# A four-layer graph network: 128-node spans at multiples of 64 for the segment sums, the tail's branch moved ahead of the last batch norm, and the routing check moved into layer 3

## The chip, the core and the metric

The kernel is one program on one core of a Trainium2 chip. Its time is the device time of one execution in microseconds (us). The core has five engines that run side by side, each on its own list of instructions in order: TensorE (PE, matmuls), VectorE (DVE), ScalarE (ACT), GpSimd (POOL), and SyncE (SP, which issues DMAs). Matmuls write PSUM, which has eight banks of 128 partitions x 512 float32 numbers; an engine must read a bank out before it is used again.

## The reference, cut to what matters

There are 3125 nodes with 256 features each and 50000 edges, sorted by destination. Four layers follow each other, and each has the same two lines:

```python
xn = layernorm(x)
x  = x + gnn(xn, edges) + mix(xn)      # a sum over the edges, and a dense mixer
x  = x + ffn(layernorm(x))             # a mixture of experts
```

- `gnn` of layer 0 sums `xn[src] @ rel_W[type]` over the edges into each destination and divides by the degree. Layer 1 is graph attention with 4 heads of 64 features: each edge's row `h[src]` is multiplied by a softmax weight before the sum. Layer 2 sums `value * h[col]`, then a batch norm over the nodes and a ReLU. Layer 3 sums `x[src]`, divides by the degree, adds a second product, makes each row's length 1, and again ends in a batch norm over the nodes and a ReLU.
- `ffn` of layer 3, called the tail here, has its own graph of 2048 nodes and 32768 edges (nodes of the first 16 tiles below). A small graph attention over it (4 heads of 4) gives scores, whose best two of four make the weights `g` of four experts: `out += g * (gelu(x @ W1[e] + b1[e]) @ W2[e] + b2[e])`, 256 to 512 to 256 features. Nodes outside of that graph get their scores without a sum.

All arithmetic is float32.

## The kernel before

**Tiles and chunks.** The nodes lie in 25 tiles of 128 (`T`; tile groups of four and a last of one, `GROUPS`). `self.x`, `self.xn` and `self.xnT` hold all nodes in SBUF. The edges lie in 391 chunks of 128 (`C1`), the tail's in 256 (`C2`). Since they are sorted by destination, the destinations of chunk c lie near node 8c.

**A segment sum.** `seg_near` (layers 0, 2 and 3) goes through the chunks. For each it issues on POOL one indirect DMA, which gathers 128 rows by their source index (L447), and for the chunk some places earlier it calls `to_tiles`. That makes on DVE a one-hot matrix E of edges by destinations (`one_hot`, L416, with the weight in it L418) and multiplies E with the gathered rows on PE (L430), adding up in a PSUM bank named `seg`, one for each node tile. `near(c)` gives the tiles in which a chunk's destinations can lie: one tile for ten chunks of each sixteen, two for the other six. With two tiles E is 128x256 and there are two matmuls. When a tile's last chunk is through, `close` reads the bank. So 391 chunks take 535 matmuls and the tail's 256 take 346. `gat_near` does the same for attention (layer 1 and the tail): its gather is L842, the softmax weights are made on DVE and ACT for sixteen chunks at a time (`att` L806, exp L834), and the gathered rows are multiplied by them in place (`ring`, L854) before the matmul. A float32 matmul has two records in the profile.

**Order.** POOL's list is in the order of the program (a manual schedule); the other engines' lists are made by a scheduler, which goes by estimated times and keeps to the dependences. `drive` interleaves generators, so many steps of each in turn: the segment sum of each layer is driven beside the layer's `mix`. `Banks` splits the eight PSUM banks among names; layer 0's and layer 1's sums have three `seg` banks, layers 2 and 3 and the tail have two.

**Batch norm.** `close` of layers 2 and 3 writes each tile's sum to DRAM (`c_h`) and adds up its statistics in `bn_tile` (L940 to L954). `bn_end` makes from them scale and shift. `bn_apply` then goes through the tile groups: it loads a group's sums into a buffer `bn_h` (L984, one buffer for each group), multiplies, adds, applies ReLU and adds to `x` on DVE (L986 to L989), and calls `norm_tiles`: statistics (L174), the reciprocal root on ACT (L139), `xn` on DVE (L178), transposes on PE and their evacuation into `xnT` (L165, L117, L119).

**Around the tail.** `route_check` tests on the device whether the tail's edges, which the kernel itself has sorted while layers 1 and 2 run, are spread evenly enough for `near`; it runs between layer 2 and layer 3. Its answer `ok` is read as a branch: `tail_regular` or `tail_general`. The branch stands after layer 3's `bn_apply`. `tail_regular` then:

- makes the experts' generator (`l3_near_ffn`, which loads the weights when it is first advanced),
- runs `breaks`, which loads each edge's neighbours in the sorted list (`dh`, sixteen small DMAs of SP, L753) and makes two masks from them (`pen`, `penc`, L755 to L761),
- runs `l3_near_setup`: the product with `W_gat` for all 25 tiles, the two attention scores of each node, a table of rows written to DRAM for the gathers (`l3rows`), and sixteen scatters on POOL that put each node's score where its first edge is (`l3seed`, L357),
- runs `spread`, which reads `l3seed` back (`sh`) and copies each score to all edges of its node (`se`, `pre`) in a scan,
- sets the weights of tile groups 16, 20 and 24, for which no sum is needed (`gate`), and takes 20 steps of the experts,
- drives the tail's `gat_near` and the experts side by side. An expert's first product (`hT`, with Gelu on ACT, L2192) needs only `xnT`; its second is added to `x` with the weight (L2200), so it waits for the group's gate. Bias rows come in after a group's four experts (L2206 to L2211). Group 12 to 15 comes last.

Two DMAs at the very end store `x` (L2625 to L2627).

**The prologue** makes all tiles' norms (`norm_x`), then the table `h_tab` group by group (`fill`), with the check of the edge list (`regular`) ahead of the fourth group's fill.

## Time and profile before

| what | value |
|---|---|
| median of 14 runs | 5123.6 us (5109.94 to 5148.38) |
| the profiled execution's own time | 5134.22 us |
| its span | 5132.4 us |
| mean granted TensorE clock | 0.812 of full speed |
| busy time, PE / DVE / ACT / POOL | 3752.1 / 2205.1 / 749.9 / 2579.8 us |
| first and last gather, layer 0 | 148.3 and 747.5 us |
| first and last gather, layer 1 | 1248.5 and 1849.9 us |
| first and last gather, layer 2 | 2399.5 and 2972.3 us |
| first and last gather, layer 3 | 3683.3 and 4332.9 us |
| first and last gather, tail | 4476.9 and 5016.6 us |

The profile is of one execution, which took 10.6 us more than the median. Its times count from the span's start. PE's busy time counts a matmul as busy at whatever clock it ran, so a stage in which the clock was low looks busier than the same work at full clock. An indirect DMA's row on POOL is the time in which POOL writes its descriptors, not the time until the data is there. "Remote" or "an unknown queue" as what ended a wait stands for a DMA's or another queue's event that the profile does not name.

### The profile page before, as it was taken

Reading aid. Unit: us, or ns where it says so; the run is one execution under the profiler, and the core shown is the slowest. Engines: PE = TensorE matmul, PEld = TensorE weight load, DVE = VectorE, ACT = ScalarE, POOL = GpSimd, SP = SyncE. Lnnn points to the kernel's source line nnn. Section 1 sums busy time; section 2 is a strip of 40 time slices with the busy share of each in tenths; the row PEclk is TensorE's granted clock in tenths of the full one; section 3 lists DMA queues with packets and bytes.
Section 4 is the critical chain, followed back from the end, with each engine's and each line's share of the span. In section 5 each row is a group of like instructions: output and inputs, shape, how many; then the busy total and the mean of one; then the engine's idle time right before and its main releaser. Section 6 shows DMA issues by size and latency. Waiting matters only on the chain.

```text
span 5132.4 us, 47098 instructions
## 1 busy us (share of the span) xinstructions
PE 3752.1 (73%) x13977; PEld 2534.5 (49%) x13977; DVE 2205.1 (43%) x7451; ACT 749.9 (15%) x1455; POOL 2579.8 (50%) x2605
## 2 busy tenths in 40 slices
PE   7778755863866766665866658998688995288888
PEld 3456543542444544343555434555465774256555
DVE  3465421125666784575434342112645222624333
ACT  2000001110100111112201011222121220012112
POOL 0475664664677635433666613662255555235440
PEclk9888876985877877877878767999798997588779
DMA  3432323213433320012333320000233233200000
GB/s 127 130 91 80 92 75 108 93 48 104 128 94 99 93 67 16 14 49 61 95 93 96 97 65 5 9 14 25 71 88 99 82 89 91 75 5 8 7 7 27
DMA packets 231200, 348.62 MB, mean 68 GB/s; under 512 B 74128, under 2 KB 168135, under 8 KB 230936
## 3 DMA queue, kind: packets, MB, share of 16 engines
q0 software_dynamic: 108384, 219.50, 15.7%
q1 hardware_dynamic: 118136, 121.97, 7.6%
q10 hardware_dynamic: 4416, 4.01, 0.2%
q8 instruction: 118, 1.93, 0.2%
q14 instruction: 146, 1.20, 0.1%
HBM read 294.62 MB, written 50.61 MB: 67 GB/s over the span
## 4 chain that ended last, share of the span: by engine, by line
PE 60%; DVE 16%; another core or an unknown queue 9%; issue 9%; DMA 3%; ACT 1%; POOL 1%; SPq 1%; DVEq 0%; POOLq 0%; ACTq 0%
PE mm L110 34%; PE seg L430 18%; DVE E L416 1%; PE mm L165 1%; DVE ring L854 1%; DVE ln_st L174 1%; PE mm L945 1%; DVE r_m L2041 1%; PE bn L954 1%; DVE xn L178 1%; PE mm L1362 1%; PE ga L812 0%; PE acc L1076 0%; DVE E L418 0%
## 5 line engine op out<-in xcount | busy, mean ns | idle before, releaser
L430 PE MATMUL seg<-G,E 128*128 128x256 f32 (+1 forms) x3210 | 886.4, 424 | 174.5 <-issue 67.2
L430 PEld LDWEIGHTS seg<-G,E 128*128 128x128 f32 x3210 | 664.1, 213 | 363.3 <-issue 151.5
L110 PE MATMUL mm<-xnT,w 128*128 128x512 f32 (+1 forms) x1232 | 554.4, 596 | 26.8 <-issue 19.7
L416 DVE TENSOR_SCALAR E<-iota_row,e1dl 128x128 f32<-128x128 f32 (+1 forms) x1173 | 363.4, 325 | 480.1 <-PE seg L430 256.1
L357 POOL DMA_INDIRECT by_src<-rec,place x391 | 395.0, 1010 | 337.0 <-PE mm L110 236.2
L447 POOL DMA_INDIRECT G<-h_tab,gi x391 | 383.4, 981 | 353.3 <-DMA selfw<-in_L_gnn_self_W 136.5
L430 PE MATMUL seg<-ring,E 128*128 128x264 f32 (+1 forms) x1762 | 450.4, 396 | 129.7 <-DVE E L416 55.3
L447 POOL DMA_INDIRECT G<-tab,e1src x391 | 379.8, 971 | 271.0 <-PE seg L430 155.7
L842 POOL DMA_INDIRECT ring<-l1rows,e1src x391 | 422.2, 1080 | 180.4 <-issue 68.3
L447 POOL DMA_INDIRECT G<-tab,e3src x391 | 387.9, 992 | 190.3 <-issue 74.5
L110 PE MATMUL mm<-w,hT 128*128 128x256 f32 (+1 forms) x1712 | 427.8, 403 | 19.2 <-ACT hT L1550 10.3
L430 PEld LDWEIGHTS seg<-ring,E 128*128 128x128 f32 x1762 | 325.3, 224 | 233.2 <-DVE E L416 82.6
L842 POOL DMA_INDIRECT ring<-l3rows,e2src x256 | 247.8, 968 | 293.0 <-PE seg L430 194.3
L357 POOL DMA_INDIRECT by_dst<-rec,place x256 | 251.6, 983 | 276.3 <-PE mm L110 213.4
L110 PEld LDWEIGHTS mm<-w,hT 128*128 128x128 f32 (+1 forms) x1712 | 328.1, 198 | 88.7 <-issue 18.9
L110 PEld LDWEIGHTS mm<-xnT,w 128*128 128x128 f32 x1232 | 241.4, 210 | 258.1 <-issue 241.2
L165 PE MATMUL mm<-ident,xn 128*128 128x128 f32 x400 | 97.1, 402 | 247.5 <-DVE xn L178 204.6
L418 DVE TENSOR_SCALAR E<-iota_row,e3dl,rec 128x128 f32<-128x128 f32 (+1 forms) x391 | 140.2, 385 | 271.1 <-PE seg L430 123.0
L1710 DVE SCALAR_TENSOR_TENSOR x<-mm,l2t_r,x 128x256 f32<-128x256 f32 x150 | 69.5, 481 | 330.3 <-PE mm L110 287.3
L165 PEld LDWEIGHTS mm<-ident,xn 128*128 128x128 f32 x400 | 68.1, 197 | 277.9 <-DVE xn L178 156.6
L854 DVE TENSOR_TENSOR ring<-ring,ex 128x260 f32<-128x260 f32 (+1 forms) x647 | 191.8, 319 | 3.5 <-ACT ex L834 2.7
L1703 ACT ACTIVATE h<-mm,b 128x512 f32<-128x512 f32 (+1 forms) x168 | 107.1, 641 | 393.6 <-PE mm L110 372.0
(710 smaller groups left out, 5096.1 us busy)
## 6 DMA issues: line engine op xcount, KB each, us to landing
w<-in_L_ffn_w SPq DMA_DIRECT2D x16, 1024.0 KB
h_tab<-htab_s SPq DMA_DIRECT2D x25, 512.0 KB
r_b<-rowa SPq DMA_DIRECT2D x64, 128.0 KB
bn_h<-c_h SPq DMA_DIRECT2D x50, 128.0 KB
G<-h_tab,gi POOLq DMA_INDIRECT x391
by_src<-rec,place POOLq DMA_INDIRECT x391
ring<-l1rows,e1src POOLq DMA_INDIRECT x391
G<-tab,e3src POOLq DMA_INDIRECT x391
```

What stands on the lines that cost most here:

```text
L110: m = self.nc.tensor.matmul(out, l, r, start=(i == 0), stop=(i == last))
L165: self.nc.tensor.transpose(p[:, i * P:(i + 1) * P], src(t0 + i)[:, k * P:(k + 1) * P], self.ident)
L174: nc.vector.bn_stats(st[:, t, :], self.x[:, t, :])
L357: return self.nc.gpsimd.indirect_dma_start(out=table, out_offset=bass.IndirectOffsetOnAxis(ap=idx, axis=0), in_=src, in_offset=None, bound ...
L416: self.nc.vector.tensor_scalar(e[:, :w], self.iota2[:, :w], g["dl"][:, c:c + 1], None, op0=OP.is_equal)
L418: self.nc.vector.tensor_scalar(e[:, :w], self.iota2[:, :w], g["dl"][:, c:c + 1], weight[:, c:c + 1], op0=OP.is_equal, op1=OP.mult)
L430: self.nc.tensor.matmul(A[t], e, rows_c, start=first, stop=last)
L447: nc.gpsimd.indirect_dma_start(out=ring[i % len(ring)][:, :D], out_offset=None, in_=table, in_offset=bass.IndirectOffsetOnAxis(ap=gidx[:, ...
L842: nc.gpsimd.indirect_dma_start(out=ring[:, i % RING].rearrange("p h f -> p (h f)"), out_offset=None, in_=table, in_offset=bass.IndirectOff ...
L854: nc.vector.tensor_mul(r[:, :, :d + 1], r[:, :, :d + 1], ex[:, c, :, None].to_broadcast([P, 4, d + 1]))
L1703: nc.scalar.activation(o[:, f, :n], p, AF.Relu, bias=b[:, 2 * e + f:2 * e + f + 1])
L1710: nc.vector.scalar_tensor_tensor(self.x[:, t, :], p, r[:, t, e:e + 1], self.x[:, t, :], op0=OP.mult, op1=OP.add)
```

## The change

1. **Spans.** `to_windows` takes the place of `to_tiles` for the sums without a weight (layers 0, 1, 3 and the tail; layer 2 stays as it is). A chunk is given one span of 128 nodes that starts at a multiple of 64 (`window`). E is always 128x128, and there is one matmul for each chunk: 391 or 256. Spans that start at a tile's first node are copied whole from PSUM to SBUF by ACT (`W_own`); those between are copied in two halves to the two tiles' `W_side`, and DVE adds own and side for every tile before `close`. A stage has 49 spans, the tail 31. The tests of the edge lists go by the same spans. Layer 0's sums have four `mm` and two `seg` banks, layer 1's two and two.
2. **Batch norm.** `bn_apply` loads into `xn` itself, and its `norm_tiles` normalises and evacuates on ACT. This holds for layers 2 and 3.
3. **The tail.** The branch now stands ahead of layer 3's `bn_end`; both arms do the batch norm themselves. In `tail_regular`, `bn_apply` takes the groups in the order 16, 20, 24, 0, 4, 8, 12, and after each group comes that group's part of the setup (`fill`: one product with a weight of 24 columns that gives the rows and both scores, ACT copies, the rows' DMA and the scatters) and, for the first three, its gate. Twelve expert steps come after the groups, forty more after `spread`. The last group's expert products do not wait for its gate: they go to `y` in `xn` with the bias, and four weighted additions for each tile follow the gate. Each group is stored when it is done.
4. **The check.** `route_check` is a third generator beside layer 3's sum and mix.
5. **The prologue** takes each group's norm just ahead of the previous group's `fill`; the check comes one group later.

The core of the diff:

```diff
+    def to_windows(self, pool, g, c, rows_c, A, w, close):
+        k = window(c, nt)
+        t = k // 2
+        nc.vector.tensor_scalar(e, self.iota_row, g["dl"][:, c:c + 1], None, op0=OP.is_equal)
...
+        nc.tensor.matmul(A["sum"], e, rows_c, start=(c == 0 or window(c - 1, nt) != k), stop=last)
...
+        if k % 2 == 0:
+            A["own"] = pool.tile([P, w], F32, name="W_own", bufs=2)
+            nc.scalar.copy(A["own"], acc)
+        else:
...
+            nc.scalar.copy(side[64:], acc[:64])
+            nc.scalar.copy(A["side"][:64], acc[64:])
+            own = A.pop("own")
+            nc.vector.tensor_add(own, own, side)
+            close(t, own)
-                self.to_tiles(pool, g, c, r.rearrange("p h f -> p (h f)"), A, 4 * f, close)
+                self.to_windows(pool, g, c, r.rearrange("p h f -> p (h f)"), A, 4 * f, close)
...
-            sums = dict(mm=3, acc=2, seg=3)
+            sums = dict(mm=4, acc=2, seg=2)
-                with Banks(self, mm=1, acc=2, ga=2, seg=3), tp("mix1") as mp:
+                with Banks(self, mm=2, acc=2, ga=2, seg=2), tp("mix1") as mp:
...
-        for t0, n in GROUPS:
-            h = pool.tile([P, n, D], F32, name=f"bn_h{t0}")
+        for t0, n in order:
+            h = self.xn[:, t0:t0 + n, :]
...
-            self.norm_tiles(t0, n)
+            self.norm_tiles(t0, n, True)
+            if then is not None:
+                then(t0, n)
...
     def tail_regular(self, sorted_r, bn, gb):
             experts = self.l3_near_ffn(fp, r, ready)
+            sc, sh = self.bn_end(bn, fp, *gb)
             pen, penc = self.breaks(gp, self.dlin2, C2)
...
+                def then(t0, n):
+                    fill(t0, n)
+                    if t0 >= T2:
+                        gate(t0, n)
+                self.bn_apply(bn, sc, sh, then, GROUPS[4:] + GROUPS[:4])
-                for _ in range(20):
+                for _ in range(12):
                     next(experts)
+            with tp("spread4") as p:
+                end(p, penc)
+            for _ in range(40):
+                next(experts)
...
-                while t0 not in ready:
+                while t0 not in ready and not last:
                     yield
...
+                    if last:
+                        nc.vector.tensor_add(y[:, e, i, :], p, b2r[:, e * D:(e + 1) * D])
...
-                with tp("chk4") as p:
-                    self.route_check(p, by_dst, ok4)
...
-                              (self.l3_mix(mp, self.xnT), 1))
+                              (self.l3_mix(mp, self.xnT), 1), (self.route_check(cp, by_dst, ok4), 1))
...
-                self.norm_x()
                 for i, (t0, n) in enumerate(GROUPS):
-                    if i == 3:
+                    self.norm_tiles(t0, n)
+                    if i:
+                        fill(*GROUPS[i - 1])
+                    if i == 4:
                         ok = self.regular(p, self.g)
-                    fill(t0, n)
+                fill(*GROUPS[-1])
```

## The prediction

> **What bounds it now.** I read the page first, then POOL's waits for each edge stage, then engine windows by stage, and for the tail the chain of waits.
>
> The page: span, the chain that ended last, and the two groups that the spans touch most (count | busy us, mean ns of one | idle before).
>
> ```profile
> span 5132.4 us, 47098 instructions
> PE 60%; DVE 16%; another core or an unknown queue 9%; issue 9%; DMA 3%; ACT 1%; POOL 1%; SPq 1%; DVEq 0%; POOLq 0%; ACTq 0%
> PE mm L110 34%; PE seg L430 18%; DVE E L416 1%; PE mm L165 1%; DVE ring L854 1%; DVE ln_st L174 1%; PE mm L945 1%; DVE r_m L2041 1%; PE bn L954 1%; DVE xn L178 1%; PE mm L1362 1%; PE ga L812 0%; PE acc L1076 0%; DVE E L418 0%
> L430 PE MATMUL seg<-G,E 128*128 128x256 f32 (+1 forms) x3210 | 886.4, 424 | 174.5 <-issue 67.2
> L447 POOL DMA_INDIRECT G<-h_tab,gi x391 | 383.4, 981 | 353.3 <-DMA selfw<-in_L_gnn_self_W 136.5
> ```
>
> PE carries 60% of the chain and segment sums 18% (0.18 x 5132 = 924 us). Two records make a matmul, so 3210 records are 3 stages x 535 matmuls, at 886.4/1605 = 0.55 us each. A gather holds POOL about 0.98 us, and 0.3 us lie before the next one (issue), so 391 cannot take less than about 391 x 1.25 = 489 us. Layer 0's gathers took 747.5 - 148.3 = 599 us, layer 1's 602, layer 3's 650: each stage is a mixture of a gather floor and of PE.
>
> POOL's waits (total us, times, longest): 148 to 760, 1248 to 1850, 3683 to 4345 and 4408 to 5060 us, in this order.
>
> ```profile
> POOL G L447 <- PE seg L430: 83.2, 88, 19.8
> ...
> POOL ring L842 <- PE seg L430: 45.4, 62, 9.0
> ...
> POOL G L447 <- PE seg L430: 155.7, 118, 8.2
> ...
> POOL ring L842 <- PE seg L430: 194.3, 36, 69.6
> ```
>
> Here gathers wait for PE to free ring buffers: layer 3 most, layer 1 little. These waits cap what fewer matmuls can give to a stage.
>
> Windows (window, length, busy us of PE, PEld, DVE, ACT, POOL, then granted clock).
>
> ```profile
> 600.00:780.00 180.00, 105.57 (x381) 81.17 (x380) 52.17 (x180) 2.93 (x12) 112.42 (x118) 0.73 0.27 76
> 3940.00:4200.00 260.00, 260.00 (x1016) 191.58 (x1015) 68.95 (x216) 69.60 (x111) 139.89 (x148) 1.00 0.29 84
> 4408.00:4526.00 118.00, 40.93 (x168) 33.98 (x168) 36.75 (x175) 7.61 (x15) 53.10 (x53) 0.57 0.25 60
> ```
>
> Layer 3's middle is PE alone (260 of 260 us at clock 1.00); layer 0's end is gathers (PE 105.6 of 180, clock 0.73); the tail's start is nobody (PE 40.9 of 118).
>
> The chain around the tail (start, us, what).
>
> ```profile
> 4339.84 4.10 PE seg L430 x19
> ...
> 4358.16 3.89 DMA bn_h<-bn_h
> ...
> 4372.50 1.28 DVE xn L178 x4
> ...
> 4421.26 6.43 DMA l3seed<-neg
> 4427.76 26.18 issue
> ...
> 4475.54 2.06 DMA l3seed<-sdst,sidx
> ...
> 4492.93 15.84 PE mm L110 x48
> 4508.77 17.26 issue
> 4526.02 13.98 PE mm L110 x37
> ```
>
> From 4349 to 4526 us the chain is latencies: batch norm, masks, a serial setup, sixteen scatters (4454 to 4475.5), the first expert, and a stop until DVE's `att` has its gathers. Then PE is busy 522 of 592 us. The profiled run is 5134.2 us (span plus 1.8), 10.6 above the median of 5123.6; I sum against 5134.2 and take 10.6 off at the end.
>
> **The change part by part.**
>
> *Spans, what they remove and add.* Each 391-chunk stage loses 144 matmuls, the tail 90. At full clock one costs 4.10/19 x 2 = 0.43 us. E shrinks, from 366 to 302 ns for those 144: DVE saves 9 us. Added per stage: 25 whole and 24 split copies on ACT, 73 in all, and 25 additions on DVE. Nearest rows: ACT 128x256 COPY from PSUM 372 ns, DVE `ring` product 319 ns; so ACT gets 27 us over 600 us, of which it used 24 of 632 in layer 0 and 59 of 602 in layer 1, and DVE 8. Both lie beside other work, unless a bank waits (rival below). Bounds of one handover: 0 to about 2 us.
>
> *Layer 0.* About 99 of the 144 matmuls fall in the first 270 chunks, where PE waits are; the rest lie in the gather-bound end. 99 x 0.48 (between 0.43 and 0.55) = 47, and I count 85%: -40. Ends: -20 (half hidden by gathers) and -60 (most of the 83.2).
>
> *Layer 1.* 391 gathers of 1.08 plus 0.3 us are 540 of 602 us. Waits for PE's sums are 45.4 and for E 10.9; I take half of the former: -22, ends -5 and -45.
>
> *Layer 3.* 107 of the 144 fall where PE is full: 107 x 0.44 = 47. The check ahead of the stage goes: POOL's first memset waited 16.5 us on `ok`. Its work now stands in the stage on DVE and PE, so I count 8 of it. Total -55, ends -30 and -75 (below half of the 155.7).
>
> *Batch norms.* A group of `bn_apply` took 7.04 us of DVE (4372.50 to 4379.14 and so on: three passes of about 1.12, four statistics, four `xn` at 0.32 spacing, `xnT` 0.69). With `xn` and `xnT` on ACT DVE keeps 5.05. Layer 2: 6.25 x 2 = 12.4 us, and a few more since loads need no closed pool: -15, ends -8 and -20. ACT takes 0.416 us for a 128x256 ACTIVATE where DVE takes 0.407: four are 1.7 and two evacuations of 0.586 1.2 us, under DVE's 5.05, which hides them. Without that cover ACT would bound the group at 2.9 us plus any table load (1.283 us in this trace), still less than 5.05.
> The Trainium skill, "ScalarE: Activation LUTs", section "Rules for kernel authors", says to use VectorE and not ScalarE for additions and products, up to three times as fast in bf16, which speaks against this step; by it the batch norm term would turn to a loss of several us. The float32 rows above (0.416 against 0.407) do not show it, so I go by the rows.
>
> *Prologue.* PE idled between the norms' transposes from 9 to 31 us, and fills now stand in there; the check (72.8 to 91 us) still follows. -5, ends 0 and -10.
>
> *Tail start.* Layer 3's end is 4349.4 us. After it SP's list has three row loads, sixteen `dh` loads (0.63 us of issue each, two buffers, so SP waits for DVE's masks, which stand behind `bn_end`) and only then the first `xn` load, behind which all groups wait. So I put DVE's first group 10 us later than now: 23 instead of 13 us after layer 3's end. Seven groups at 5.05 are 32 us, against 4407 now: about even. The gain comes behind that: masks, `W_gat`'s product (4424 to 4445), `neg` (6.4), `sidx` (4453.7) and most of the scatters now lie beside the groups. Twelve scatters can go under the groups, four follow (4 x 1.3), then the round trip of `l3seed` and `sh` (2 + 5.5) and the scans. First gather about 4442 instead of 4476.9: -35, ends 0 (SP's list holds everything) and -50. Behind the waiting `att` on DVE stand the experts' additions, as now; so PE stops again until gather 35 (46 us after the first), but two experts (15.8 + 13.8) are done by then, not one: -14.
>
> *Tail, rest.* 90 matmuls fewer: the small ones took 0.31 us (108.3 us for 346), at 0.27 for the part at full clock -24. Last group's bias steps (5113.1 to 5118.9) shrink to four short additions on DVE: -4. PE's idle 71 of 592 us, with the gate stall of 4 at 5065: -12, ends 0 and -25. Final store 5118.9 to 5132.4, 13.5 us for 3072 KB, becomes 128 KB: near the 3.9 us of the `bn_h` load, so -9. Tail: -35 - 14 - 24 - 4 - 12 - 9 = -98, ends -60 and -135.
>
> *Sum.* -5 - 40 - 22 - 15 - 55 - 98 = -235. 5134.2 - 235 = 4899; less 10.6, 4889 us by the median. Sum of the ends: -123 and -345, that is 5000 and 4779.
>
> A second rule speaks against the spans. The Trainium skill, "TensorE: Matmul & The Clock Gate", section "Part 1: The HAM clock gate", says the array runs at half clock after an idle window of some 3.4 us. The windows agree in kind (clock 1.00 at 3940 to 4200, 0.73 at 600 to 780). By the rule alone, PE with less to do in the gather-bound parts idles more and the saving there is eaten; the terms above already take little there.
>
> **Rivals.**
>
> *Gathers take over.* PE's waits shrink, but the queue's own time and the gathers' latency show up in their place: "an unknown queue" is 9% of the chain, and 47% of it in layer 0's last 180 us. Then layers 0, 1 and 3 give -20, -5 and -30, and the tail without an earlier start -60: with -20 in the prologue and layer 2 -135, 4989 us. Against it: the 155.7 and 83.2 us of waits on PE.
>
> *Slower: evacuation holds the banks.* Two `seg` banks, and ACT frees them in order behind Gelu (0.687 us), Exp batches with table loads (1.283 us) and statistics. If a span's bank is late, PE's whole list stands, experts and mixer with it. 3 x 49 + 31 = 178 spans. The saving of 235 is used up from 235/178 = 1.3 us a span, a queue of two Gelus or one load on ACT each time; at 2 us a span (356 us) the kernel is 121 slower, 5245 us. For it: ACT's list is shared with the mixers, 35.2 of 200 us busy at 3740 to 3940. Against it: ACT is 15% busy, and a span lasts eight chunks, some 10 us, while only one bank is being read.
>
> *The tail does not move.* The list on SP, and the experts behind all norms, make its start as late as now or 10 us later; then -98 becomes about -45, the total -182, 4942 us.
>
> *It does not do what it says.* A span test that fails sends the program to the general arms, far slower. With the reference's inputs the sorted destinations of each chunk of 128 lie 0 to 115 nodes behind their span's start (0 to 127 in the tail), so the tests should hold; 1 in 100.
>
> **Chances.** Forecast 0.62 (4830 to 4950), the tail alone not moving 0.12, gathers taking over 0.14, banks and other losses 0.11, general arm 0.01. A measurement of this kernel can tell about 0.2%, 10 us. Faster by more: 0.62 + 0.12 + 0.14 = 0.88; of the 0.12 left I give 0.01 to the same and 0.11 to slower. The range reaches from near the better ends (4800) to just past the gather rival (5005); outside are the two losing cases and a little at each end.
>
> **What would show it.** Right: 391 and 256 matmuls a stage in the sums' groups; POOL's waits on `seg` at a third of now in layer 3, with that stage 45 to 60 us shorter and layer 1's only some 20; first tail gather about 93 us after the last batch norm matmul of layer 3 (127 now); two experts done ahead of `att`; the last chain piece a small store. Wrong: PE's `seg` waiting for ACT copies by the span; layer 0 still near 599 us; the first `xn` load over 30 us after layer 3's end; or a layer 1 that lengthens because its additions on DVE delay the `ring` products.

## The result, and the profile after

The changed kernel takes 5160.9 us (median of 10 runs, 5150.92 to 5186.44); the kernel before, in the 47 runs that go with them, 5122.23 us. The ratio is 1.0085, interval 1.0065 to 1.0104: slower by 39 us, where 4889 us, a gain of 235, had been forecast. The profiled execution took 5171.95 us at a mean clock of 0.793.

The page of the changed kernel: the span, the chain by engine, and the two groups that answer to those shown of before.

```profile
span 5170.2 us, 45299 instructions
PE 55%; DVE 18%; another core or an unknown queue 11%; issue 10%; DMA 3%; ACT 2%; POOL 0%; SPq 0%; DVEq 0%; ACTq 0%; POOLq 0%
L459 PE MATMUL seg<-G,E 128*128 128x257 f32 (+1 forms) x1564 | 473.7, 443 | 202.0 <-DVE E L455 83.7
L494 POOL DMA_INDIRECT G<-tab,e1src x391 | 379.8, 971 | 507.7 <-PE seg L459 230.0
```

The matmuls are gone as announced: 1564 records are 782 matmuls for layers 0 and 3, 391 each, and the group costs 473.7 us. PE's share of the chain fell from 60% to 55%. The time went elsewhere: "an unknown queue" rose from 9% to 11%, DVE from 16% to 18%, and layer 3's gathers now wait on `seg` far longer than before. POOL's waits in the four edge stages show that (layer 0, layer 1, layer 3, tail; total us, times, longest):

```profile
POOL G L494 <- PE seg L459: 89.5, 80, 18.1
...
POOL ring L892 <- PE seg L459: 57.6, 73, 11.6
...
POOL G L494 <- PE seg L459: 230.0, 104, 21.6
...
POOL ring L892 <- PE seg L459: 144.4, 32, 26.8
```

Before, these were 83.2, 45.4, 155.7 and 194.3. Fewer matmuls did not shorten the first two. In layer 3 the wait grew by 74 us and its longest one from 8.2 to 21.6 us. Windows of the stretches that answer to those of before:

```profile
600.00:780.00 180.00, 101.33 (x290) 66.02 (x288) 50.39 (x184) 11.28 (x34) 108.48 (x115) 0.65 0.26 72
3940.00:4200.00 260.00, 212.62 (x720) 144.89 (x721) 51.14 (x175) 63.68 (x110) 106.89 (x113) 0.88 0.23 65
4384.00:4487.00 103.00, 54.23 (x196) 39.24 (x196) 62.89 (x262) 35.58 (x87) 22.73 (x25) 0.54 0.37 105
```

In layer 0's end PE did less and was granted less clock (0.65 against 0.73). In layer 3's middle, where PE had been busy 260 of 260 us, it is busy 212.6 of 260 at clock 0.88: PE now stands idle in a stretch where it had been busy throughout. The tail's start (layer 3's end to the first gather) is 103 us of mixed work instead of 118.

The stages, first to last gather and what lies between, in the two profiled executions:

| stretch | before, us | after, us | change | forecast |
|---|---|---|---|---|
| to the first gather | 148.3 | 136.0 | -12.3 | -5 |
| layer 0 gathers | 599.2 | 601.0 | +1.8 | -40 |
| up to layer 1 | 501.0 | 505.4 | +4.4 | 0 |
| layer 1 gathers | 601.3 | 607.0 | +5.7 | -22 |
| up to layer 2, layer 2 gathers | 1122.5 | 1122.1 | -0.4 | 0 |
| batch norm, experts, check, up to layer 3 | 710.9 | 666.2 | -44.7 | -15 - 8 |
| layer 3 gathers | 649.6 | 728.3 | +78.7 | -47 |
| up to the tail's first gather | 144.0 | 116.3 | -27.7 | -35 |
| tail gathers | 539.7 | 593.5 | +53.8 | -14 - 24 - 12 |
| last gather to the end | 115.8 | 94.5 | -21.3 | -4 - 9 |

Four stretches gain 106 us together, layer 3 and the tail's gathers lose 132, layers 0 and 1 give nothing.

The experiments came in five calls, each on one chip, and the chips are of two kinds. On that of the result and that of calls 2 and 3 (one chip; before: 5122, 5069 and 5073 us) PE's signals to the other engines often come late: of the signals that the trace records, 18% in after and 15% in before arrive over 1 us after the start of the last matmul record that sends one. On those of calls 1, 4 and 5 (three chips; before: 4596, 4597 and 4593 us) that share is 0.5 to 0.7%. They are called late and prompt chips below.

What the engines do takes the same time on both kinds: a gather 0.95 us and 0.30 us to the next, a run of twelve chunks on PE 5.34 us (shown below for after and h_after), a DMA packet during layer 3's gathers 0.118 us on average in after and 0.114 in h_after. What differs is when a waiting engine goes on. The mean granted clock differs too (before: 0.81 to 0.82 on late chips, 0.85 to 0.86 on prompt ones). The share of late signals is a rough measure: the traces of late chips record only 84 to 87% of PE's signals and 70 to 76% of DVE's and ACT's, those of prompt chips over 99%. So on a late chip "issue" or "remote" can also stand for a release that was not recorded.

### The profile page after: what moved, and what is told of

Read it like the earlier page. It is cut to its first block, busy times and chain, and to the rows that moved or that the text cites. A ratio compares the mean times of both kernels' runs of the same rounds, so it can differ in the third digit from the quotient of the medians.

```text
span 5170.2 us, 45299 instructions
## 1 busy us (share of the span) xinstructions
PE 3613.1 (70%) x12927; PEld 2352.3 (45%) x12927; DVE 2167.5 (42%) x7507; ACT 879.5 (17%) x1815; POOL 2586.3 (50%) x2609
## 4 chain that ended last, share of the span: by engine, by line
PE 55%; DVE 18%; another core or an unknown queue 11%; issue 10%; DMA 3%; ACT 2%; POOL 0%; SPq 0%; DVEq 0%; ACTq 0%; POOLq 0%
PE mm L116 33%; PE seg L459 10%; PE seg L443 4%; DVE E L455 2%; DVE ring L904 1%; PE mm L171 1%; DVE ln_st L180 1%; PE mm L995 1%; DVE r_m L2093 1%; PE bn L1004 1%; PE ga L862 1%; PE mm L1414 1%; DVE r_oha L2052 0%; DMA G<-h_tab,gi 0%
## 5 line engine op out<-in xcount | busy, mean ns | idle before, releaser
L459 PE MATMUL seg<-G,E 128*128 128x257 f32 (+1 forms) x1564 | 473.7, 443 | 202.0 <-DVE E L455 83.7
L116 PE MATMUL mm<-xnT,w 128*128 128x512 f32 (+1 forms) x1232 | 567.6, 610 | 23.0 <-issue 14.2
L455 DVE TENSOR_SCALAR E<-iota_row,e1dl 128x128 f32<-128x128 f32 x1173 | 325.1, 298 | 533.3 <-PE seg L459 237.8
L892 POOL DMA_INDIRECT ring<-l1rows,e1src x391 | 434.2, 1110 | 174.3 <-issue 79.9
L459 PE MATMUL seg<-ring,E 128*128 128x264 f32 (+1 forms) x1294 | 387.6, 429 | 188.5 <-DVE E L455 84.6
L459 PEld LDWEIGHTS seg<-G,E 128*128 128x128 f32 x1564 | 325.7, 220 | 331.0 <-issue 150.1
L459 PEld LDWEIGHTS seg<-ring,E 128*128 128x128 f32 x1294 | 247.2, 239 | 305.6 <-DVE E L455 123.6
L443 PE MATMUL seg<-G,E 128*128 128x256 f32 x1070 | 296.0, 425 | 74.4 <-issue 36.0
L443 PEld LDWEIGHTS seg<-G,E 128*128 128x128 f32 x1070 | 223.3, 214 | 133.2 <-issue 53.1
## 6 DMA issues: line engine op xcount, KB each, us to landing
h_tab<-htab_s SPq DMA_DIRECT2D x25, 512.0 KB
```

What stands on the lines that cost most here:

```text
L116: m = self.nc.tensor.matmul(out, l, r, start=(i == 0), stop=(i == last))
L443: self.nc.tensor.matmul(A[t], e, rows_c, start=first, stop=last)
L455: nc.vector.tensor_scalar(e, self.iota_row, g["dl"][:, c:c + 1], None, op0=OP.is_equal)
L459: nc.tensor.matmul(A["sum"], e, rows_c, start=(c == 0 or window(c - 1, nt) != k), stop=last)
L892: nc.gpsimd.indirect_dma_start(out=ring[:, i % RING].rearrange("p h f -> p (h f)"), out_offset=None, in_=table, in_offset=bass.IndirectOff ...
```

## The experiments

| run | ratio to before (95%) | L0 | L1 | L3 | tail gathers |
|---|---|---|---|---|---|
| *late chips* | | | | | |
| c_before | 1 | 593.2 | 599.2 | 646.1 | 529.9 |
| c_after | 1.0054 (1.0037 to 1.0071) | 598.5 | 592.6 | 699.5 | 584.2 |
| c_after2 | 1.0033 (1.0008 to 1.0059) | 608.6 | 595.9 | 707.9 | 581.9 |
| f1_no_spans_l3_tail | 0.9907 (0.9878 to 0.9937) | 599.6 | 603.3 | 655.1 | 567.0 |
| f2_l3_ring8 | 1.0061 (1.0036 to 1.0086) | 604.1 | 594.5 | 726.8 | 578.0 |
| f3_experts_20 | 0.9917 (0.9893 to 0.9941) | 608.9 | 598.5 | 701.7 | 538.6 |
| *prompt chips* | | | | | |
| e1_no_spans | 0.9842 (0.9826 to 0.9859) | 512.0 | 555.8 | 596.7 | 485.6 |
| e2_no_spans_l3 | 0.9898 (0.9882 to 0.9915) | 512.1 | 564.6 | 596.8 | 489.9 |
| e3_no_spans_tail | 0.9831 (0.9802 to 0.9860) | 512.7 | 569.5 | 567.7 | 484.0 |
| e4_dve_evac | 0.9943 (0.9927 to 0.9960) | 525.1 | 597.4 | 581.7 | 490.6 |
| g1_l3_pauses | 0.9842 (0.9826 to 0.9858) | 515.7 | 565.5 | 569.6 | 490.4 |
| g2_no_spans_l3_tail_exp20 | 0.9875 (0.9855 to 0.9895) | 512.4 | 569.3 | 596.4 | 474.5 |
| g3_no_spans_exp20 | 0.9811 (0.9794 to 0.9827) | 512.2 | 554.4 | 594.6 | 474.3 |
| g4_spread_first | 0.9853 (0.9837 to 0.9870) | 517.3 | 570.7 | 565.1 | 504.0 |
| h_after | 0.9844 (0.9815 to 0.9873) | 516.9 | 565.1 | 565.1 | 489.3 |
| h1_l3_pauses | 0.9850 (0.9833 to 0.9866) | 516.5 | 568.4 | 571.6 | 489.8 |
| h2_l3_pauses_long | 0.9859 (0.9833 to 0.9886) | 516.7 | 570.0 | 577.4 | 490.6 |
| h3_no_spans_exp20 | 0.9821 (0.9804 to 0.9837) | 511.1 | 551.9 | 598.0 | 477.9 |

### Call 1: which stage's spans lose

Three kernels put the old sums (`to_tiles`, E up to 128x256) back, in all stages with the old banks in layers 0 and 1, in layer 3 alone, or in the tail alone; the fourth keeps the spans and lets DVE empty the banks.

```diff
# e1 all stages, e2 layer 3 (seg_near without count), e3 tail (gat_near with n == C2)
-                    self.to_windows(pool, g, c, ring[c % len(ring)], A, w, close)
+                    self.to_tiles(pool, dict(g, dl=g["dt"]), c, ring[c % len(ring)], A, w, close)
# e1 also
-            sums = dict(mm=4, acc=2, seg=2)
+            sums = dict(mm=3, acc=2, seg=3)
# e4
-            nc.scalar.copy(A["own"], acc)
+            nc.vector.tensor_copy(A["own"], acc)
-            nc.scalar.copy(side[64:], acc[:64])
-            nc.scalar.copy(A["side"][:64], acc[64:])
+            nc.vector.tensor_copy(side[64:], acc[:64])
+            nc.vector.tensor_copy(A["side"][:64], acc[64:])
```

> The changed kernel with part 1 undone: to_tiles and the old banks again in layers 0, 1, 3 and the tail; everything else as changed. Stage lengths from the two profiles (first to last gather): layer 0 599.2 before, 601.0 after; layer 1 601.4 and 607.0; layer 3 649.6 and 728.2; tail 539.7 and 593.5. Theory A (the spans themselves lose the time, in layer 3 and the tail): layer 3 back near 650, the tail's gathers near 540, total about 5161 - 79 - 54 - 7 = 5021 us. Theory B (the other parts lose it: the check as a third generator in layer 3, the tail's new order): layer 3 stays near 728 or grows by the 62 us of matmuls put back, the tail near 594, total 5160 or more.

> The changed kernel with to_tiles in layer 3 alone. Theory A: layer 3's gathers from 728 to about 650 us, total about 5161 - 79 = 5082. Theory B (the check as a third generator): layer 3 stays at 728 or above, total 5160 to 5200. The rest should not move by more than 10 us in either.

> The changed kernel with to_tiles in the tail alone. Theory A: the tail's gathers from 594 to about 540 us, total about 5107. Theory B (the tail's new order of experts and attention): tail near 594 or up to 24 us longer for the 90 matmuls, total 5160 to 5185. Layer 3 stays at 728 in both.

> The changed kernel with the spans' PSUM copies on DVE in place of ACT. Theory A1 (the spans lose because ACT, in order behind Gelu and table loads, hands the banks and the sums over late): layer 3 from 728 to below 680, total below 5110. Theory A2 (the spans lose because fewer matmuls let POOL issue its gathers in long runs, 16 in a row in layer 3's last phase where there were 9, and everything that waits for PE in such a run is late): PE's order is the same, so layer 3 stays within 15 us of 728 and the total within 20 us of 5161.

The expectations were written with the late chip's lengths and cannot decide between their theories here, since the call fell on a prompt chip. All four are faster than before, by 0.6 to 1.7%; the changed kernel was not in this call, and h_after in call 5, on another prompt chip, gives its place there, 0.9844. Read with it, layer 3 without spans takes 597 us and with them 565 to 568: there the spans gain some 30 us, in the direction of the forecast. Layer 0 takes 511 to 512 us without spans in any stage and 512 to 517 with them. Layer 1 is 9 to 19 us longer with the spans and their banks (565 to 571 against 552 to 556), the tail 4 to 6 us. In sum the spans are worth nothing that can be told here: e1 without them has the ratio of h_after with them, so the 75 us that h_after gains come from the rest of the change. DVE in ACT's place (e4) costs layer 1 another 32 us and layer 3 some 16, so ACT's evacuation is not what has to be taken away. Most of layer 1's loss lies in the gathers' own rows on POOL, whose mean is 1.10 us in e1, 1.12 in h_after and 1.18 in e4: over 391 gathers 9 us more in h_after, and 24 more again in e4. Why they lengthen was not tested.

### Call 2: the same two kernels on a late chip

No edit: the changed kernel, and the kernel before, each with a profile, since call 1 had run on a chip on which before takes 4596 us and not 5122.

> [...] Theory L (late signals: on the first chip what waits for PE is released several us late while POOL issues gathers in long runs, and the change makes these runs longer): where no signal is late the forecast's mechanism shows and the changed kernel is faster than before, ratio about 0.98, layer 3 near 568 us, the tail near 490, the same as in the run without spans in the tail alone. Theory O (PE's order itself loses the time): ratio above 1.00, since the order is the same on every chip.

> The kernel before, for its trace on the chip of this call. Theory L: layer 0's gathers about 512 us, layer 1's about 560, layer 3's about 600, the tail's about 490 if this is the second chip; 599, 601, 650 and 540 if it is the first.

The signals are late on this chip as well, so the call does not decide between theories L and O. The loss is there again, 1.0054, and it lies in the same stages: layer 3 +53 us and the tail's gathers +54, layer 0 +5, layer 1 -7. With h_after (0.9844, call 5) the sign depends on the chip, and what has to be explained is layer 3 and the tail.

### Call 3: what cures the loss where it shows

```diff
# f1: to_tiles in layer 3 and the tail (as in e2 and e3)
# f2: a ring of 8 gathers in layer 3 instead of 16
-                        drive((self.seg_near(gp, g, tab, g["src"], self.l3_close(gp, own, bn)), 2),
+                        drive((self.seg_near(gp, g, tab, g["src"], self.l3_close(gp, own, bn), ahead=4), 2),
# f3: 20 expert steps behind spread, none ahead of it
-                for _ in range(12):
-                    next(experts)
             with tp("spread4") as p:
                 end(p, penc)
-            for _ in range(40):
+            for _ in range(20):
                 next(experts)
```

> The changed kernel with to_tiles in layer 3 and the tail, spans in layers 0 and 1. On a chip with late signals (before at 5070 to 5130 us), theory L (spans lengthen the gathers' runs, and so the stretches in which PE's signals are late): layer 3's gathers back from 700 to 728 to about 648 us, the tail's from 584 to 594 to about 540, total 100 to 130 us below the changed kernel, ratio to before about 0.98. Theory O (the tail's order and the third generator in layer 3): both stages stay, ratio 1.005 or more. On a chip without late signals both theories give layer 3 about 597 and the tail about 486.

> The changed kernel with 8 gather buffers in layer 3 in place of 16 (ahead=4), so that after PE's pauses POOL can issue 8 gathers in a row at most and not 16. Theory L with late signals: fewer signals are late in layer 3's last phase, so layer 3 gets shorter than 700 by 20 us or more although the buffers are fewer. Theory O or plain buffering: fewer buffers let POOL and PE wait for each other more often, layer 3 longer than 700, by up to 100 us. Without late signals only the second effect is there.

> The changed kernel with 20 expert steps behind spread in place of 12 ahead of it and 40 behind. Theory O for the tail (52 steps taken early are missing later as cover for the attention's chain): the tail's gathers from 584 to 594 back towards 540 us, the start as late as now or a little earlier, total 20 to 50 us below the changed kernel. Theory L for the tail: the stage from first to last gather stays within 15 us of 584 to 594 where signals are late, and the total is 0 to 30 us above the changed kernel, since two experts are no longer done while the first gathers run.

> The changed kernel again as the control of this call. With late signals: ratio to before 1.00 to 1.01, layer 3 700 to 728, tail 584 to 594. Without: ratio 0.98 to 0.985, layer 3 about 568, tail about 490, by theory L.

f1 is 64 us below c_after2 (5026.42 against 5090.4) and beats before by 0.9%. Its layer 3 is back at 655 us. A window in the middle of that stage, and POOL's wait on the sums over it:

```profile
3860.00:4060.00 200.00, 200.00 (x768) 144.97 (x767) 53.49 (x168) 56.20 (x90) 109.53 (x115) 1.00 0.29 85
```

```profile
POOL G L494 <- PE seg L443: 158.1, 123, 13.9
```

PE is busy 200 of 200 us at full clock, as in the kernel before, and the wait is 158.1 us, before's 155.7. The part of the change that loses in layer 3 is therefore the spans. In the tail f1 gains less than expected: its gathers take 567 us where about 540 had been named, and the total falls by 64 us and not by 100 to 130.

Where in the stage: from the first to the last Gelu of the mixer's products (`m`, the time in which PE has other work than sums) before takes 278 us with 3.5 us of PE idle, c_before 277 with 2.1, f1 277 with 2.1; after takes 351 with 69.4, c_after 326 with 47.3, c_after2 324 with 50.8. The idle time follows one hand-over. In the same phase each tile's batch norm statistics go from PE's `mm<-c_h,ones` to ACT's `bn_r`, 0.4 us when nothing is late; what the 25 tiles take beyond 0.42 us adds up to 14.2 us in before, 8.2 in c_before, 4.3 in f1, and to 69.2 in after, 49.7 in c_after and 57.8 in c_after2. The share of PE's signals that are over 1 us late is 9 to 10% in layer 3 of before, c_before and f1, and 14 to 20% in after, c_after, c_after2 and f3 (10% in f2). In the phase alone it is 1.0 to 1.5% in the first three and 11 to 21% in the next four (8% in f2). So on the same late chip the lateness in this phase comes with the spans; so do long runs of gathers without a break, which hold 141 to 151 of the phase's some 165 gathers with the spans (131 in f2) and 5 or 6 without. In h_after the runs are there (144) and no signal is late.

The timeline shows one such stretch of the changed kernel on the late chip (start, us, engine, line; in brackets the idle time before and its releaser):

```profile
4030.53 5.34 PE L459 MATMUL seg<-G,E 128*128 128x256 f32 x24
...
4039.16 0.29 DVE L455 TENSOR_SCALAR E<-iota_row,e1dl 128x128 f32<-128x128 f32 x1 [2.13 <-issue]
4039.37 0.35 DVE L1813 TENSOR_SCALAR c_h<-c_h,c_s 128x256 f32<-128x256 f32 x1
...
4039.77 1.22 PE L995 MATMUL mm<-c_h,ones 128*128 128x256 f32 x2 [3.90 <-issue]
...
4042.70 0.37 ACT L465 COPY W_own<-seg 128x256 f32<-128x256 f32 x1 [7.79 <-PE mm L116]
4042.70 0.29 DVE L455 TENSOR_SCALAR E<-iota_row,e1dl 128x128 f32<-128x128 f32 x1 [2.99 <-PE mm L116]
```

PE has twelve chunks' sums in a row (24 records; ten chunks in the kernel before), done at 4035.87. The next thing in its list is a batch norm product that needs `c_h` from DVE, and DVE comes to `c_h` only at 4039.37, behind an E that stood 2.13 us for which the profile names no releaser. So PE stands 3.9 us. ACT's copy of the next span, of a sum that lies in that run of 24, and DVE's next E both start at 4042.70, 6.8 us after the run's end: two engines released at one moment, late.

f2 decides little: the ring of 8 left most of the pattern of gathers as it was (131 of the phase's gathers in unbroken runs of ten or more, 141 to 151 with the ring of 16), and PE's idle time too, 50.5 us. Layer 3 is 19 us longer than in c_after2.

f3 leaves layer 3 as it is and takes 54 us from the kernel, in the tail: 538.6 us of gathers against 581.9. That is near what theory O had named (gathers near 540, 20 to 50 us in all), and not theory L's 0 to 30 us of loss. The first `att` comes 26.7 us after the first gather, 57.2 in c_after2, 59.0 in after, 26.3 in before. The chain of the changed kernel at that place:

```profile
4471.13 12.84 PE mm L116 x32
4484.68 32.08 another core or an unknown queue
4517.47 9.81 issue
```

And the timeline behind the two long entries:

```profile
4483.99 0.69 ACT L2264 ACTIVATE hT<-mm,b 128x512 f32<-128x512 f32 x1 [1.03 <-PE mm L116]
...
4489.96 1.55 DVE L824 TENSOR_TENSOR_SCAN se<-penc,sh 64x672 f32<-64x672 bf16 x1 [0.18 <-issue]
...
4490.70 3.60 PE L116 MATMUL mm<-xnT,w 128*128 128x512 f32 x8
...
4516.79 0.69 ACT L2264 ACTIVATE hT<-mm,b 128x512 f32<-128x512 f32 x1 [32.10 <-remote]
...
4517.57 0.34 PE L827 MATMUL mm<-ident,se 64*128 64x64 f32 x1 [7.70 <-issue]
...
4528.02 0.36 PE L827 MATMUL mm<-ident,se 64*128 64x64 f32 x1 [10.11 <-ACT hT L2264]
...
4533.90 1.55 DVE L824 TENSOR_TENSOR_SCAN se<-penc,sh 64x672 f32<-64x672 bf16 x1 [27.86 <-PE mm L827]
```

The 12 steps of experts stand ahead of `spread` in PE's list. `spread` scans on DVE (`se`), PE transposes, DVE scans again. The first scan is done at 4491.5, but its transposes come at 4517.57 and 4528.02, because PE's list holds experts' products ahead of them, whose banks Gelu must empty. ACT stood 32.1 us before its next Gelu at 4516.79, though the products for it had run from 4490.70 to 4494.30: they had ended 22 us before. The second scan starts at 4533.90 after 27.9 us. In f3 `spread` stands ahead:

```profile
4425.30 1.55 DVE L824 TENSOR_TENSOR_SCAN se<-penc,sh 64x672 f32<-64x672 bf16 x1 [11.63 <-DMA ring<-l3rows,e2src]
...
4427.06 0.66 PE L827 MATMUL mm<-ident,se 64*128 64x64 f32 x4 [14.36 <-DMA ring<-l3rows,e2src]
4427.75 1.55 DVE L824 TENSOR_TENSOR_SCAN se<-penc,sh 64x672 f32<-64x672 bf16 x1 [0.90 <-PE mm L827]
```

Scan, transposes, scan: 2.5 us from start to start where it was 43.9. But the order alone does not cost this. h_after has the same twelve steps ahead, on a prompt chip:

```profile
3935.70 7.03 PE L116 MATMUL mm<-xnT,w 128*128 128x512 f32 x16
...
3937.61 0.69 ACT L2264 ACTIVATE hT<-mm,b 128x512 f32<-128x512 f32 x1 [7.94 <-PE mm L116]
...
3942.66 0.40 PE L827 MATMUL mm<-ident,se 64*128 64x64 f32 x3
```

Here the Gelu follows the start of its products by 1.9 us, where it was 26.1, PE goes from the products to the transposes at once, and `att` comes 27.0 us after the first gather. So the wait takes both, the steps ahead of `spread` and a late release. Of the 43 us that f3 takes from the tail's gathers 30.5 are the earlier `att`. The rest is not separated: f3 also has 32 early steps fewer in all, and no run on a late chip changes the place alone or the number alone.

### Call 4: does breaking the run of gathers help, and do f1 and f3 add up

Two theories were left for layer 3. L: PE's signals are late while gathers follow each other closely. P: PE's new order, twelve sums in a row, is itself the loss.

```diff
# g1: a GpSimd fill of 128x128 behind layer 3's gathers 140 to 329
+                if pause and 140 <= i < 330:
+                    nc.gpsimd.memset(rest, 0.0)
# g2: f1 and f3 together; g3: e1 and f3 together
# g4: all 52 steps behind spread
-                for _ in range(12):
-                    next(experts)
...
-            for _ in range(40):
+            for _ in range(52):
```

> The changed kernel with a POOL memset of 128x128 after each of layer 3's gathers 140 to 329 (its output is not used), so that a gather in a long run takes some 1.7 us and not 1.25; PE's order is that of the changed kernel. Where signals come late (layer 3's MLP phase of the mixer 324 to 351 us for the changed kernel, 277 without spans; PE idle in it 47 to 69 us against 2; bn_r on ACT follows its matmul by 0.4 us or, in long runs, by 4 to 8, summing to 50 to 69 us over the tiles). Theory L (PE's signals are late because POOL issues gathers back to back): slower gathers make the sum fall below 25 us and the MLP phase below 300. Theory P (PE's own order, 12 chunks in a row, is what loses it): order unchanged, so the phase stays at 320 or above, and gets longer by the slower gathers.

> No spans in layer 3 and the tail, and 20 expert steps behind spread: the two edits that each gave about 60 us (f1: 64, f3: 54 below the changed kernel of that call). If the two losses are separate: about 5090 - 64 - 43 = 4983 us where before takes 5073, ratio 0.982; layer 3 about 650, the tail about 530. If they overlap (one lateness shared): ratio 0.987 to 0.99. On a chip without late signals: ratio 0.98 to 0.985.

> As g2, and to_tiles with the old banks in layers 0 and 1 too, so that nothing of part 1 is left. Layer 0 and layer 1 from first to last gather were 593 to 609 and 593 to 607 us with and without spans. If the gathers bound them: both stages within 10 us of g2, total within 10 us of g2. If the spans help there by the forecast's 40 and 22 us: g3 about 60 us above g2.

> The changed kernel with its 52 early expert steps all behind spread, none ahead of it. In the changed kernel att follows the first gather of the tail by 57 to 59 us on the chips with late signals, by 27 with the experts behind spread (f3) and by 27 on the other chip. Theory L (the 12 steps ahead stand on PE, ACT and DVE in front of spread's scans, and their signals are late while the first 35 gathers run): att after about 27 us and the tail's gathers at 550 to 560. Theory C (52 early steps are too many, so that cover is missing later): the gathers stay at 575 to 590 us.

This call fell on a prompt chip, so it could not show the cure: g1's phase takes 250.9 us with 0.8 of PE idle, with nothing left to mend. The fill was a weak test besides. It takes 0.22 us but lies mostly in the gap that is there anyway: in the runs a gather follows the one before after 1.34 us and not after 1.25, where 1.7 had been expected.

What the call does show is the rest of the tail. Without spans in the tail its gathers take 474 us with 20 steps ahead of the sums (g2, g3) and 484 to 486 with 12 and 40 (e3, e1). With spans they take 489 with 12 and 40 (h_after) and 504 with all 52 behind `spread` (g4). So on prompt chips fewer early steps are better, and moving all 52 behind `spread` is worse, although `att` comes after 26 to 27 us in all of them.

g2 (0.9875) misses the 0.98 to 0.985 expected without late signals: its layer 3 has lost the spans' gain. g3 is 33 us below g2, where 10 us either way or 60 above had been named: 15 us of it are layer 1's gathers (554.4 against 569.3), and most of the rest lies between the layers' sums and is not explained. g3 has the best ratio of all, 0.9811.

### Call 5: the fills beside their control

```diff
# h1 as g1; h3 as g3; h_after is the changed kernel
# h2: the fill twice as wide
-            rest = pool.tile([P, P], F32, name="rest")
+            rest = pool.tile([P, 2 * P], F32, name="rest")
```

> The changed kernel with one GpSimd fill of 128x128 (0.22 us in g1) behind each of layer 3's gathers 140 to 329, as in g1, here beside the changed kernel itself. Theory L (PE's signals come late while gathers follow each other closely): the mixer's product phase of layer 3 (324 to 351 us in three profiles of the changed kernel) falls by 15 us or more, PE's idle time in it (47 to 69 us) falls to below 35, and layer 3 (700 to 728 us) to below 690. Theory P (PE's order of twelve sums in a row, with the batch norm's matmul behind it, is itself the loss): nothing changes but by the fills, within 8 us. On a chip on which the changed kernel shows no such idle time (g1: 0.8 us) both give no change.

> As h1 with fills of 128x256, about 0.44 us by double of g1's 0.22. Theory L: PE's idle time in the product phase falls further than in h1, below 25 us, unless the gathers themselves become the bound: 165 gathers of 0.97 + 0.30 + 0.44 us are 282 us, so the phase cannot fall below that. Theory P: no change, or longer by up to 10 us.

> No spans in any stage, and twenty expert steps behind the spread instead of twelve ahead and forty behind (as g3, 0.9811 on its chip). If what f1 and f3 gave adds up (64 and 54 us of the changed kernel's 5090 on one chip): about 118 us below the changed kernel, ratio to the kernel before near 0.98. If both cured the same late start of the tail: no more than 80 us below, 0.988. Layer 3 near 650 us, tail gathers near 520, att some 27 us after the tail's first gather.

> The changed kernel again as the control of h1 and h2. On a chip like those of c_after and c_after2: 1.003 to 1.006, layer 3 near 700 us. On a chip like that of e1 to e4: layer 3 near 568 us as in e3, tail near 486 us as in e1, so about 4519 + 1 us, ratio 0.983 to 0.985: a gain on that chip and a loss on the other, by the same code.

Again a prompt chip. h1 and h2 change nothing that can be told (0.9850 and 0.9859 beside 0.9844), as both theories expected there. The fills stretch a gather's cadence from 1.25 us to 1.34 and 1.44 (the wider fill takes 0.33 us, not 0.44); whether gaps between gathers cure the late signals has not been measured where signals are late. h3 is 9 us below h_after; the 80 to 118 us named for it were for a late chip, and so were its layer 3 near 650 us and tail near 520 (598 and 478 here). h_after is the run that counts: the same instructions in the same order as in the result gain 1.6% here, 4517.88 against 4592.95 us. A window of its layer 3's middle:

```profile
3480.00:3680.00 200.00, 199.81 (x761) 143.98 (x760) 55.25 (x192) 68.84 (x120) 116.17 (x123) 1.00 0.31 92
```

```profile
POOL G L494 <- PE seg L459: 107.0, 155, 8.7
```

PE is busy 199.8 of 200 us, and POOL's wait on `seg` over the stage is 107.0 us instead of 230.0. The same stretch as in the timeline above, one tile of the same phase on this chip:

```profile
3480.09 5.34 PE L459 MATMUL seg<-G,E 128*128 128x256 f32 x24
...
3484.97 0.34 DVE L1813 TENSOR_SCALAR c_h<-c_h,c_s 128x256 f32<-128x256 f32 x1
3485.04 0.37 ACT L465 COPY W_own<-seg 128x256 f32<-128x256 f32 x1 [0.56 <-PE seg L459]
...
3485.37 0.70 PE L995 MATMUL mm<-c_h,ones 128*128 128x256 f32 x2
```

The twelve chunks end at 3485.43; DVE's `c_h` is ready at 3484.97 while they run, ACT copies the next span at 3485.04 and PE never stops. So twelve sums in a row with the batch norm product behind them (theory P) are no loss by themselves: over the whole phase this order leaves 0.5 us of PE idle here and 47 to 69 us on the late chips. It takes the late signals as well. Both runs of twelve chunks take 5.34 us, so neither PE's clock nor the products' own time makes the difference there.

## Why the prediction was wrong

The main step that failed is the price of the spans: -40, -22, -47 and -24 us, from matmuls that go away where PE was taken for the limit. Measured, layers 0 and 1 gain nothing (+1.8 and +5.7), layer 3 loses 78.7 and the tail's gathers lose 53.8. The kernel that had been profiled ran on a late chip, and the forecast took the time it saw there for PE's work.

**Layer 0 (-40, measured +1.8).** The step that failed is "99 x 0.48", PE's time as the stage's limit because POOL waits for PE. On the prompt chips layer 0 with 535 matmuls (e1) takes 512.0 us with 387 of its 390 gaps between gathers at the bare 0.30 us, and h_after with 391 matmuls 516.9: the stage lies near the gathers' floor, 391 x (0.98 + 0.30) = 500 us, and POOL's waits on `seg` in it are 57.0 us in the one and 56.4 in the other. So the 83.2 us of waits on `seg` were not a price of matmuls. Part of each is the plain 0.30 us (88 x 0.30 = 26). On the late chips, where the stage takes 593 to 609 us with either number of matmuls, 26% of PE's signals in before and a third in after are over 1 us late in this stage; that the rest of the wait comes from them is argued, not shown. With 144 matmuls fewer the wait is 89.5. The forecast had named "layer 0 still near 599 us" as a sign of being wrong, and it came, at 601.0. The rival that gathers take over described this stage and layer 1, but was priced at half of the gain, not at none.

**Layer 1 (-22, +5.7).** The same step. On prompt chips this stage too lies near the gathers' floor: 391 x (1.10 + 0.30) = 547 us at e1's mean, which takes 555.8, and 391 x (1.12 + 0.30) = 555 at h_after's, which takes 565.1; the spans with their banks add 9 to 19 us there. On the late chips c_after is 7 us below c_before, so no sign is shown.

**Layer 3 (-55, of which -47 the spans).** On prompt chips the step holds in kind: 597 to 565 us, -31. On the late chips it is +79 (+53 in call 2). The failed assumption is in "107 of the 144 fall where PE is full": it treats PE's list as work only. Fewer matmuls let twelve chunks follow each other where it was ten, and PE then reaches the batch norm's product before its input is there; with signals that come 6 to 8 us late PE stands 47 to 69 us. The phase of the mixer's products has +72.8 us of the stage's +78.7, the stretch ahead of it +14.3 and the one behind it -8.5. Moving the check did about what was forecast: from the last `self3s` to the first gather 20.7 us became 4.4, and the stretch ahead of the phase takes 264 us in f1, with the check in it and no spans, against 255 in c_before on the same chip. That is 16 gained and 9 lost, where 8 in all had been counted.

**Slower, by evacuation.** The rival named the right side and the wrong mechanism. PE waited for the span copies' release hardly at all; these are the only entries of that kind in PE's waits between the first and last gathers (layer 1, then layer 3):

```profile
PE seg L459 <- DVE W_own L474: 0.5, 2, 0.2
...
PE seg L459 <- ACT W_own L465: 0.9, 1, 0.9
```

That is 1.4 us by name; one more wait of 5.4 us stands at 763 us, behind layer 0's last gather. In h_after, whose signals are nearly all recorded, they sum to 3.0 us. The rival needed 1.3 us for each of 178 spans. ACT's copies come late, but because they are released late. The sign that I had named, "PE's `seg` waiting for ACT copies by the span", is absent, and e4 loses more.

**Batch norms (-15) and check.** Right: from layer 2's last gather to the router's product `mm<-rw,rh` 77.4 us became 61.9, -15.5, and a group of `bn_apply` takes 5.15 us of unbroken work on DVE (10.30 for two) where it took 7.04. One row was mis-sized: `xn` on ACT takes 0.588 us in after (50 rows) and not the 0.416 of another form, against 0.407 on DVE. So the rule of the Trainium skill, "ScalarE: Activation LUTs", section "Rules for kernel authors", that sends additions and products to VectorE, agrees with the single rows; the step gains all the same because DVE's list was the longer one and ACT's work lies beside it. The other 29 us of that stretch are the check (-16.3) and 13.0 us in the experts that were not forecast and are not explained here.

**The clock gate.** The Trainium skill, "TensorE: Matmul & The Clock Gate", section "Part 1: The HAM clock gate", expects an idle PE to lose its clock, and the windows agree: 0.73 to 0.65 in layer 0's end, 1.00 to 0.88 in layer 3's middle. In layer 3 it looks like a consequence of PE standing: f1, whose PE is busy, has 1.00 again.

**Tail start (-35, -27.7).** About right, and by its mechanism: the first gather comes 97.9 us after layer 3's last batch norm matmul (about 93 forecast, 127 before). **Two experts ahead (-14).** The step that failed: I counted the products that would be done and not that `spread`, which `att` needs, stands behind them in PE's list, with hand-overs to ACT between. On the late chip `att` came 33 us later than before, and f3 undoes it; on the prompt one (h_after) the same order costs nothing. **90 matmuls fewer (-24)** and **PE's idle time (-12).** PE's idle time between the tail's first and last sum went from 63.0 to 132.8 us; f1 leaves 85.0, f3 85.4. On prompt chips the spans cost the tail 4 to 6 us and save none. **Bias and store (-13, -21.3).** The right sign, a little small. **Prologue (-5, -12.3).** Just outside of its bounds, on the good side.

So four stretches gain 106 us in these profiles, and 100 from c_before to c_after; what the forecast had for the rest turned into two losses on late chips and into about nothing on prompt ones. Why PE's signals are late on some chips, and whether gathers that follow each other closely make them later, stays open: the share of late signals rises within a run of gathers in after (some 6% at 2 to 4 us, some 25% at 10 to 12), but it is some 20% outside of such runs too, and the fills that were to tell it ran only on prompt chips. Whether the recording of the trace itself has a part in it is not tested either: the chips whose signals come late are those whose traces lack signals.

The best version was the one without spans and with 20 expert steps behind `spread`: 0.9811 and 0.9821 of before on two prompt chips (g3, h3). In h3's call the changed kernel has 0.9844 and the intervals overlap, so there it surely beats before, and the changed kernel only by the medians, 4509.25 against 4517.88 us. On late chips its two halves were each measured, f1 and f3, 64 and 54 us below the changed kernel; both together were not.

## What to carry to other kernels

A wait of POOL on PE is not PE's throughput until the wait's size is compared with what PE does in it: many short waits of one issue gap are a gather floor, and long ones may be signals. Before pricing work that is moved ahead on an in-order engine, follow what stands behind it in that list, and ask whose hand-over it takes to get past it: the same order cost 30 us on one chip and nothing on another. Time the same program on more than one chip before a verdict of a per cent: here the sign changed.

## What was not expected of the hardware

- The kernel before takes 10 to 12% longer on late chips (4593 to 4597 against 5069 to 5122 us), and the changed kernel's ratio to it goes from 0.9844 to 1.0085, with one gather at 0.95 us and the gap behind it at 0.30 us on all.
- PE's recorded signals are over 1 us late in 13 to 18% of cases on the one kind of chip and in 0.5 to 0.7% on the other; of those of DVE and ACT that the traces of before, after and h_after record, 2.1% and less are. In the changed kernel's tail a Gelu started 22 us after the products it needs had ended.
- A POOL fill of 128x128 (0.22 us) put between two gathers lengthens their cadence by 0.09 us only, from 1.25 to 1.34 (g1, h1).
